# Two-layer graph kernel: transposed exponentials in pairs of groups, a regrouped opening, and other queues and spacing at the start of layer 1

## The chip, the cores and the metric

The kernel runs on one core of one Trainium2 chip. Its engines run side by side and wait for one another by semaphores: TensorE (PE; its weight loads are listed as PEld), VectorE (DVE), ScalarE (ACT), GpSimd (POOL) and SyncE (SP), which here mostly issues DMAs. The metric is the device time of a whole execution in microseconds (us), lower is better.

## What is computed

There are 2708 nodes with 256 features and a dense matrix adj, about as sparse as a random graph. Two layers follow each other, each with a residual and a layernorm. Cut to what matters:

```python
# layer 0, two steps n = 0, 1
A  = softmax(Xa @ W1.T @ W2.T @ (Xa @ W3.T).T)      # N x N
A  = keep the largest entries of each row up to a mass of 0.9, rescale
R  = (adj + I) / row sum
Xf = R @ Xf
Xa = A @ Xa
Z  = Z + Xf @ U1[n].T + Xa @ U2[n].T
h  = layernorm(x + Z) * ln_g + ln_b
x  = layernorm(x + h)
# layer 1, four heads of 64
Wh = x @ W                                          # per head
e  = leaky_relu(s_i[:, None] + s_j[None, :])        # s = Wh @ a, per head
p  = softmax(e where adj or the diagonal is nonzero)
x  = layernorm(x + p @ Wh)
```

All of it is in float32.

## The kernel before

**Tiles.** The 2708 rows are 22 tiles, 16 of 128 rows and 6 of 110. For transposes they are put into six groups: four of four tiles of 128, one of four and one of two tiles of 110 (`groups`, L75).

**The attention of layer 0.** One tile of target rows has its exponentials e in an array of 128 x 2708. To multiply them with the values, each 128 x 128 block has to be turned. `turned` (L235) transposes the blocks of one group on TensorE into a PSUM buffer `tr` (L240) and has ScalarE copy them to `eT` (L245). `weigh` (L248) runs over the six groups of a target tile: it first turns the group after the present one, then issues the present group's matmuls (L258, one for each source tile), then calls `between`, in which all other work is put. After the last group, group 0 of the next target tile is turned. The PSUM pool ps_tr, from which `tr` comes, has two buffers, used in turn, and it is used for other things as well: the turned rows of the next X (L644), the projections to queries and keys (`project`, L631, emptied at L635 and L636), `terms2` (L960, products with U, emptied by ScalarE at L965 and L966), and `sources` (Wh and s for layer 1, L160 to L176). ScalarE thus empties nearly every buffer of ps_tr, in the order of its program.

**What sets the order.** Inside the layers the order is written out by hand: every engine executes its instructions in the order in which the program issues them. `slot` (L999) is called once for each group of each target tile. It advances every running search by one stage (`going`), starts the search of target tile t + 3 at one place of the tile, advances the unfinished follow-up work (`doing`), and then spends some matmuls of the "walks" (R @ Xf, L901). A search computes a tile's scores (L661), its exponentials (L665), tallies over them on ScalarE (L686), and on DVE the threshold of the 0.9 mass, ending with the masked e.

**The stages.**
- Opening: `turn_x` (L1080) turns the groups of x by TensorE into PSUM, in two halves c = 0, 1 of the features (L1086). After each half a copy empties it (L1091), ScalarE for c = 0, DVE for c = 1. `project` (L631) then makes queries and keys of the group. The group after it is turned ahead of each projection. Then come `terms1` for all tiles (L946) and the first searches.
- Step 0: attention of 22 tiles; `spend` is 0, so there are no walks beside it. Follow-up work of a tile is L644, on odd tiles a projection of two tiles, and `terms2`.
- Between: 15 slots (L1117 to L1121) with seven walk matmuls each; the first searches of step 1 are started. The last source of each walk tile sets DVE's sum xf (L915).
- Step 1: attention of 22 tiles with six or seven walk matmuls after each group (SPEND_1, L37). Follow-up work is the layernorms and `sources`, which stores v, the scaled Wh, to memory.
- Layer 1: target tiles in three spans of 8, 8 and 6 tiles, sources j in pairs. `neighbours` (L1214) loads a block of adj and makes a 0/1 mask on ScalarE (Sign L1221, Square L1222). `weights` has DVE make the four heads' products pt (L1302), `values` and `denominators` are the matmuls (L1313, L1323). `mask` (L1286) also loads v of a source tile, in the first span only, through SP's queue (L1290).
- Late tiles: the last four tiles (LATE) are not finished in layer 0. `prepared` (L1330) carries their layernorm and `sources` on beside the first pairs of layer 1. `beside` is called twice for each pair of source tiles; an entry `[k, part]` of `late` lets k calls pass before its first stage, and then does one stage per call. `verdict`, which checks that the threshold search was valid, follows them; a general path behind it is not run.

**Memory.** SBUF tiles come from pools; a pool's place is taken from another's after that is closed. The pools of layer 1 lie where those of layer 0 lay, so their first use waits for the last use of what was there.

Of the kernel before, what the change touches and what calls it, by code (L numbers as in the profile page):

```python
# [8 lines left out]
F32 = mybir.dt.float32  # L9
# [7 lines left out]
P = 128  # L17
# [17 lines left out]


SPEND_BETWEEN, SPEND_1 = 7, (7, 6, 7, 7, 6, 7)  # L37
HELD, WAITING = 6, 4
LN2 = 0.6931471805599453

Z_LOW, Z_HIGH = 1e-25, 1e30
# [3 lines left out]
def kernel(  # L45
# [16 lines left out]
    nc = tc.nc  # L62
    N, D = x.shape
# [4 lines left out]
    NT = (N + P - 1) // P  # L68

    rows = [P] * 16 + [110] * 6  # L70
# [177 lines left out]
    def weigh(acc, ahead, m, value, turn_next, between=None):  # L248

        for n, grp in enumerate(groups):
            eT, ahead = ahead, turn_next(n + 1)
            for q, t in enumerate(grp):
                nc.tensor.matmul(  # L258
                    acc, eT[: rows[t], q, :m], value(t),
                    start=(t == 0), stop=(t == NT - 1),  # L260
                )
            if between:
                between(n)
        return ahead


    def general_layer0():
        with ExitStack() as l0:
# [18 lines left out]
            keep = l0.enter_context(tc.tile_pool(name="keep", bufs=1))  # L287
            ep = l0.enter_context(tc.tile_pool(name="ep", bufs=2))
            wk = l0.enter_context(tc.tile_pool(name="wk", bufs=1))
            tpp = l0.enter_context(tc.tile_pool(name="tpp", bufs=4))  # L290
            adjp = l0.enter_context(tc.tile_pool(name="adjp", bufs=2))
            ps_lg = l0.enter_context(tc.tile_pool(name="ps_lg", bufs=2, space=PSUM))
            ps_tr = l0.enter_context(tc.tile_pool(name="ps_tr", bufs=2, space=PSUM))
# [142 lines left out]
            def attend(t, e, rden, cur, dst):  # L436

                m = rows[t]
                ac = ps_ac.tile([P, CHUNK], F32, name="ac")

                def turn_next(n):
                    return turned(e, m, n, tpp, ps_tr, nc.scalar.copy) if n < len(groups) else None

                weigh(ac[:m, :D], turn_next(0), m, lambda j: cur[: rows[j], j, 0:D], turn_next)
                nc.scalar.activation(dst, ac[:m, :D], AF.Copy, scale=rden[:m])

            def walk(s, t, dst):
# [77 lines left out]
    def fast_layer0(ep, adjp):  # L525

        l0 = ExitStack()

        heldp, finp, rowp, w0, keep, tpp, sortp, keepb, wk = (
            l0.enter_context(tc.tile_pool(name=name, bufs=bufs))  # L530
            for name, bufs in (
                ("heldp", HELD), ("finp", 2), ("rowp", 2), ("w0", 1), ("keep", 1),
                ("tpp", 3), ("sortp", 1), ("keepb", 1), ("wk", 1),
            )
        )
        ps_lg, ps_wk, ps_at, ps_tr = (
# [317 lines left out]
        def walks():  # L854

            queue = [
                (s, t, j0, j1)  # L860
                for s in range(STEPS) for t in range(NT) for j0, j1 in ((0, HT), (HT, NT))
            ]

            def load(s, t, j0, j1):
                m = rows[t]
                blk = adjp.tile([P, NT - HT, P], F32, name="blk")
                if (s, t) < (0, 2):

                    nc.gpsimd.memset(blk[:, :, 0:1], 0.0)
                by_tile(blk[:, :, :m], adjT[:, off[t] : off[t + 1]], j0, j1)  # L870
                return blk

            blocks = [load(*queue[0]), load(*queue[1])]
            yield
            for n, (s, t, j0, j1) in enumerate(queue):
                m = rows[t]
                cur, w = (xe, D + 1) if s == 0 else (xm, D)
                while s and unfinished:
                    yield True
                blk = blocks.pop(0)  # L880
                if n + 2 < len(queue):
                    blocks.append(load(*queue[n + 2]))
                if j0 == 0:
                    ac = ps_wk.tile([P, CHUNK], F32, name="walk")
                    if s and t >= NT - LATE:
                        ca = x_late[:, t - NT + LATE, :]
                        nc.gpsimd.memset(ca[:, 0:1], 0.0)
                    else:
                        ca = finp.tile([P, D], F32, name="ca", bufs=4)
                    if s:  # L890
                        cb = finp.tile([P, D], F32, name="cb")
                        nc.sync.dma_start(ca[:m], x[off[t] : off[t + 1], :])
                        nc.sync.dma_start(cb[:m], c2[t][:m])
                        if t in c3:
                            assert t in stored
                            held[t] = finp.tile([P, D], F32, name="cc")
                            nc.sync.dma_start(held[t][:m], c3[t][:m])
                    else:
                        nc.sync.dma_start(ca[:m], c1[t][:m])
                for j in range(j0, j1):  # L900
                    nc.tensor.matmul(  # L901
                        ac[:m, :w], blk[: rows[j], j - j0, :m], cur[: rows[j], j, 0:w],
                        start=(j == 0), stop=(j == NT - 1),
                    )
                    if j == NT - 1:
                        doing.append(after_walk0(t, ac, ca) if s == 0 else finish(t, ac, ca, cb))
                        next(doing[-1])
                    yield j == NT - 1
# [103 lines left out]
        def step(s, cur, spend):  # L1012
            first = None
            for t in range(NT):
                m = rows[t]
                e, rden = ready[t]
                ac = ps_at.tile([P, CHUNK], F32, name="att")
                if s == 0 and t == NT - 1:
                    next(stream)
                if s and t == NT - 2:  # L1020
                    share(0, ps_tr.tile([P, 4, P], F32, name="tr"))
                if s and t == NT - 1:
                    ahead.extend(room(ep))
                    spread(0, ahead)

                def between(n):
                    last = n == len(groups) - 1
                    if last:
                        xa = heldp.tile([P, D], F32, name="xa1")
                        nc.scalar.activation(xa[:m], ac[:m, :D], AF.Copy, scale=rden)  # L1030
                        if s and t in c3:
                            nc.gpsimd.dma_start(c3[t][:m], xa[:m])
                            stored.add(t)
                        elif s:
                            held[t] = xa
                        else:
                            doing.append(after_attention0(t, xa))
                    slot(spend[n], (s, t + 3) if n == len(groups) - 2 else None)

                def turn_next(n):  # L1040
                    u = t + n // len(groups)
                    if u == NT:
                        return None
                    return turned(ready[u][0], rows[u], n % len(groups), tpp, ps_tr, nc.scalar.copy)

                first = weigh(
                    ac[:m, :D], first or turn_next(0), m,
                    lambda j: cur[: rows[j], j, 0:D], turn_next, between,
                )
                ready.pop(t)  # L1050
# [29 lines left out]
        def turn_x(grp):  # L1080
            k = rows[grp[0]]
            w, c0 = k * len(grp), off[grp[0]]
            tp = ps_lg.tile([P, 2, CHUNK], F32, name="lg")
            for c in range(DC):
                for q, t in enumerate(grp):
                    nc.tensor.transpose(  # L1086
                        tp[:, c, q * k : (q + 1) * k], xm[:k, t, c * P : (c + 1) * P],
                        ident[:k, :k],
                    )
                copy = nc.vector.tensor_copy if c else nc.scalar.copy  # L1090
                copy(x_turned[:, c, c0 : c0 + w], tp[:, c, :w])  # L1091
            return c0, w

        with tc.manual_schedule(engines=engines):
# [22 lines left out]
            for t in range(3):  # L1117
                for n in range(6):
                    slot(SPEND_BETWEEN, None if n else (1, t))
                    if (t, n) == (2, 2):  # L1120
                        break  # L1121
            step(1, ba, SPEND_1)
            owed[0] = 0
# [69 lines left out]
    def layer1(ep, adjp, r=None, verdict=None):  # L1193
        l1 = ExitStack()

        pp, pj, rp, keep = (
            l1.enter_context(tc.tile_pool(name=name, bufs=bufs))
            for name, bufs in (("pp", 2), ("pj", 1), ("rp", 1), ("keep1", 1))
        )
        DEEP = 3  # L1200
        ps_u = l1.enter_context(tc.tile_pool(name="ps_u", bufs=2, space=PSUM))
# [84 lines left out]
        def mask(n):  # L1286
            if n < len(order):
                g, _, j = order[n]
                if g == 0:
                    nc.sync.dma_start(  # L1290
                        v[j][: rows[j]].rearrange("p h o -> p (h o)"), vd[j][: rows[j]]
                    )
                masks[n] = neighbours(g, j)
# [44 lines left out]

        late = []
        if verdict:  # L1340
            late += [[k, prepared(NT - LATE + k)] for k in range(LATE)]
            late.append([LATE, verdict(aux)])
        rest, running = [], []
        def beside(g, i):

# [128 lines left out]
```

## Time and profile before

| | us |
|---|---|
| median of 3 runs | 1595.95 (1595.8 to 1597.88) |
| the profiled execution's own time | 1593.14 |
| its span, first to last instruction | 1591.3 |
| mean granted TensorE clock | 0.990 of full |

Stages of the profiled execution, from the busy time of windows of the trace (us; the limits are read from the timeline):

| stage | window | PE busy | DVE busy | ACT busy |
|---|---|---|---|---|
| opening | 0 to 34 | 20.9 | 8.1 | 6.8 |
| terms1, first searches | 34 to 80 | 46.0 | 30.5 | 22.4 |
| step 0 | 80 to 448 | 366.8 | 248.9 | 157.5 |
| between | 448 to 523 | 69.4 | 40.4 | 36.7 |
| step 1 | 523 to 1229 | 704.4 | 558.7 | 390.6 |
| layer 1, first pairs | 1229 to 1312 | 75.8 | 72.0 | 40.5 |
| layer 1, the rest | 1312 to 1591 | 259.0 | 243.9 | 144.5 |

The waits of TensorE by what ended them, from the view of waits: L1086 for ScalarE's copy L1091 6.4 us in 6 waits; L901 for DVE's L915 5.0 in 3; L166 for ScalarE's L162 3.8 in 2; L1313 for the DMA of v 2.2; L631 for ScalarE's L636 1.6 in 2; L160 for ScalarE's L153 1.1; each of the others is at most 1.0 us, except those for the first weights.

How to read it: a line of the timeline is start, duration, engine, line of the kernel, operation, output<-inputs, shape, count, and in brackets how long the engine had been idle and which instruction released it. Busy times of matmuls overlap (a matmul's record lasts longer than the time to the next one's start), so times per matmul are taken from start to start. Two records stand for each float32 matmul.

### The profile page before, as it was taken

The numbers are of one execution on the slowest core, as the hardware profiler recorded it, in microseconds if no ns is written. First come the engines' busy times: TensorE is split into PE (matmuls) and PEld (weight loads), VectorE is DVE, ScalarE is ACT, GpSimd is POOL, SyncE is SP. The second block draws the span as 40 slices with busy tenths as digits, with TensorE's granted clock in tenths as the row PEclk, the third lists the DMA queues.
The fourth block names the chain that finished last, engine by engine and source line by source line (L and its number), as shares of the span: only waits on it lengthen the run. The fifth ranks groups of instructions, "written<-read, shape, count | busy, mean of one in ns | idle before, by whom it ended". The sixth has DMA issues, their size and how long they took to land. (4 is left out here: it accounts for less than half of the span.)

```text
span 1591.3 us, 23822 instructions
## 1 busy us (share of the span) xinstructions
PE 1542.3 (97%) x8029; PEld 1037.7 (65%) x8029; DVE 1202.5 (76%) x3651; ACT 798.9 (50%) x1462; POOL 429.1 (27%) x884
## 2 busy tenths in 40 slices
PE   6999999999998999999999999999999999999994
PEld 3477777777776888787787788887787333333342
DVE  2777677767408876878779888888884978999995
ACT  2444444444335455555555556556643454456473
POOL 1311000000022222232224454534441720033133
PEclk9999999999999999999999999999999999999997
DMA  5200000000134333333333334433344434334331
GB/s 139 78 13 14 12 9 12 10 9 10 42 94 124 86 100 82 98 76 78 80 102 94 100 107 107 111 104 93 78 101 130 130 102 139 93 105 133 85 100 43
DMA packets 172494, 128.27 MB, mean 81 GB/s; under 512 B 44342, under 2 KB 161804, under 8 KB 172362
## 3 DMA queue, kind: packets, MB, share of 16 engines
q1 hardware_dynamic: 165030, 114.63, 26.9%
q0 software_dynamic: 3648, 9.26, 1.8%
q10 hardware_dynamic: 3684, 2.76, 0.5%
q8 instruction: 65, 1.06, 0.3%
q14 instruction: 67, 0.55, 0.1%
HBM read 111.78 MB, written 13.46 MB: 79 GB/s over the span
## 5 line engine op out<-in xcount | busy, mean ns | idle before, releaser
L245 ACT COPY eT<-tr 128x512 f32<-128x512 f32 (+5 forms) x264 | 141.2, 535 | 275.8 <-PE tr L240 273.1
L686 ACT ACTIVATE junk<-e,minus,rth 128x2708 bf16<-128x2708 f32 (+1 forms) x88 | 232.8, 2646 | 36.1 <-POOL rth L718 35.2
L258 PE MATMUL att<-xm,eT 128*128 128x256 f32 (+3 forms) x968 | 230.9, 380 | 0.4 <-ACT xa L1030 0.4
L258 PE MATMUL att<-ba,eT 128*128 128x256 f32 (+3 forms) x968 | 230.8, 379 | 0.3 <-ACT eT L245 0.2
L901 PE MATMUL walk<-xe,blk 128*128 128x257 f32 (+3 forms) x968 | 225.3, 384 | 5.0 <-DVE xf L915 5.0
L901 PE MATMUL walk<-xm,blk 128*128 128x256 f32 (+3 forms) x968 | 222.0, 380 | 1.0 <-DVE xw L974 1.0
L1313 PE MATMUL acc<-pt,v 128*64 128x512 f32 (+3 forms) x1056 | 216.3, 555 | 2.4 <-DMA v<-v 2.2
L901 PEld LDWEIGHTS walk<-xe,blk 128*128 128x128 f32 (+3 forms) x968 | 178.5, 187 | 50.3 <-issue 12.6
L1302 DVE SCALAR_TENSOR_TENSOR pt<-e,tj,blk 128x1024 f32<-128x1024 f32 (+3 forms) x176 | 187.1, 1128 | 20.3 <-PE att L258 8.7
L901 PEld LDWEIGHTS walk<-xm,blk 128*128 128x128 f32 (+3 forms) x968 | 177.7, 186 | 34.5 <-issue 4.9
L258 PEld LDWEIGHTS att<-xm,eT 128*128 128x128 f32 (+3 forms) x968 | 169.6, 186 | 22.1 <-ACT xa L1030 0.8
L258 PEld LDWEIGHTS att<-ba,eT 128*128 128x128 f32 (+3 forms) x968 | 169.5, 186 | 22.0 <-ACT eT L245 0.8
L665 ACT ACTIVATE e<-lg 128x1024 f32<-128x1024 f32 (+1 forms) x132 | 121.0, 921 | 110.6 <-PE lg L661 107.0
L1313 PEld LDWEIGHTS acc<-pt,v 128*64 128x64 f32 (+1 forms) x1056 | 75.6, 139 | 133.2 <-issue 107.5
L766 DVE MAX8 cand<-e 128x8 f32<-128x170 f32 (+1 forms) x352 | 89.6, 323 | 90.5 <-ACT e L665 90.4
L240 PEld LDWEIGHTS tr<-ident,e 128*128 128x128 f32 (+3 forms) x968 | 115.1, 138 | 56.3 <-issue 21.0
L240 PE MATMUL tr<-ident,e 128*128 128x128 f32 (+3 forms) x968 | 147.1, 271 | 0.7 <-ACT xe L952 0.3
L1302 DVE SCALAR_TENSOR_TENSOR pt<-r,tj,blk 128x1024 f32<-128x1024 f32 (+1 forms) x88 | 110.0, 1313 | 5.8 <-PE acc L1323 3.0
L1323 PE MATMUL acc<-pt,sb 128*32 128x512 f32 (+3 forms) x1056 | 106.8, 545 | 0.0
L766 DVE MAX8 cand<-scr 128x8 f32<-128x97 f32 (+1 forms) x616 | 102.3, 245 | 0.0
L1221 ACT ACTIVATE blk<-blk 128x1024 f32<-128x1024 f32 (+3 forms) x66 | 63.1, 956 | 70.2 <-DMA blk<-in_adjT_dram 57.1
L915 DVE TENSOR_TENSOR xf<-walk,xe 128x257 f32<-128x257 f32 (+1 forms) x22 | 9.4, 426 | 110.8 <-PE walk L901 110.8
(237 smaller groups left out, 1976.2 us busy)
## 6 DMA issues: line engine op xcount, KB each, us to landing
blk<-in_adjT_dram SPq DMA_DIRECT2D x32, 704.0 KB
blk<-in_adjT_dram SPq DMA_DIRECT2D x32, 512.0 KB
blk<-in_adjT_dram SPq DMA_DIRECT2D x48, 330.0 KB
blk<-in_adjT_dram SPq DMA_DIRECT2D x32, 320.0 KB
blk<-in_adjT_dram SPq DMA_DIRECT2D x12, 605.0 KB
blk<-in_adjT_dram SPq DMA_DIRECT2D x12, 440.0 KB
blk<-in_adjT_dram SPq DMA_DIRECT2D x18, 283.6 KB
c<-cs POOLq DMA_DIRECT2D x32, 128.0 KB, 2.0
```

The lines of the kernel that those rows point to most:

```text
L240: nc.tensor.transpose(tr[: rows[t], q, :m], e[:m, off[t] : off[t + 1]], ident[:m, :m])
L245: copy(eT[:k, : len(grp), :m], tr[:k, : len(grp), :m])
L258: nc.tensor.matmul(acc, eT[: rows[t], q, :m], value(t), start=(t == 0), stop=(t == NT - 1),)
L665: nc.scalar.activation(halves[:m, :, c0 : c0 + w], lg[:m, :, :w], AF.Exp, accum_out=zp[:m, n : n + 1],)
L686: nc.scalar.activation(junk[:m], e[:m], func, scale=rth, bias=minus1[:m], accum_out=acc)
L766: nc.vector.max(cand[:, n, :], src[:m, n * size : min(N, (n + 1) * size)])
L901: nc.tensor.matmul(ac[:m, :w], blk[: rows[j], j - j0, :m], cur[: rows[j], j, 0:w], start=(j == 0), stop=(j == NT - 1),)
L915: nc.vector.tensor_add(xf[:m], ac[:m, : D + 1], xe[:m, t, :])
L1221: nc.scalar.activation(bar, bar, AF.Sign)
L1302: nc.vector.scalar_tensor_tensor(pt[:k, :gw], targets[g][h // 2][:k, h % 2, :gw], tj[:k, j, h : h + 1], bar, op0=ALU.max, op1=ALU.mult,)
L1313: nc.tensor.matmul(acc[h // 2][c][q * FO : (q + 1) * FO, :w], v[j][:k, h, :], probs[n][h][:k, c0 : c0 + w], **at,)
L1323: nc.tensor.matmul(acc[2][c][h * 32 : (h + 1) * 32, :w], sb[:k, j, h : h + 1].to_broadcast([k, 32]), probs[n][h][:k, c0 : c0 + w], **at,)
```

## The change

It does six things.

1. `weigh` turns two groups at once: at every even n the groups n + 2 and n + 3, while the matmuls use the two that were turned before. The order on TensorE is thus eight transposes, a group's matmuls and its `between`, the next group's matmuls and its `between`. Both callers pass a list of two. The pool tpp (eT) has four buffers instead of three; ps_tr keeps two. HELD is 5 instead of 6, and `ca` has three buffers instead of four.
2. Searches of t + 3 begin at group len(groups) − 3 instead of len(groups) − 2, and the between phase has 16 slots instead of 15.
3. `turn_x` issues the transposes of both halves before both copies.
4. Layer 1 loads v through ScalarE's queue instead of SP's.
5. The late tiles start 2k calls of `beside` late instead of k, and the verdict 2 * LATE instead of LATE.
6. The order of pools in memory changes: tpp stands after rowp in layer 0, and rp before pj in layer 1.

```diff
-HELD, WAITING = 6, 4
+HELD, WAITING = 5, 4
...
         for n, grp in enumerate(groups):
-            eT, ahead = ahead, turn_next(n + 1)
+            if n % 2 == 0:
+                now, ahead = ahead, [turn_next(n + 2), turn_next(n + 3)]
+            eT = now[n % 2]
             for q, t in enumerate(grp):
                 nc.tensor.matmul(
...
-        heldp, finp, rowp, w0, keep, tpp, sortp, keepb, wk = (
+        heldp, finp, rowp, tpp, w0, keep, sortp, keepb, wk = (
             l0.enter_context(tc.tile_pool(name=name, bufs=bufs))
             for name, bufs in (
-                ("heldp", HELD), ("finp", 2), ("rowp", 2), ("w0", 1), ("keep", 1),
-                ("tpp", 3), ("sortp", 1), ("keepb", 1), ("wk", 1),
+                ("heldp", HELD), ("finp", 2), ("rowp", 2), ("tpp", 4), ("w0", 1),
+                ("keep", 1), ("sortp", 1), ("keepb", 1), ("wk", 1),
             )
         )
...
-                        ca = finp.tile([P, D], F32, name="ca", bufs=4)
+                        ca = finp.tile([P, D], F32, name="ca", bufs=3)
...
-                    slot(spend[n], (s, t + 3) if n == len(groups) - 2 else None)
+                    slot(spend[n], (s, t + 3) if n == len(groups) - 3 else None)
...
-                    ac[:m, :D], first or turn_next(0), m,
+                    ac[:m, :D], first or [turn_next(0), turn_next(1)], m,
                     lambda j: cur[: rows[j], j, 0:D], turn_next, between,
...
-                copy = nc.vector.tensor_copy if c else nc.scalar.copy
+            for c, copy in enumerate((nc.scalar.copy, nc.vector.tensor_copy)):
                 copy(x_turned[:, c, c0 : c0 + w], tp[:, c, :w])
...
-                    if (t, n) == (2, 2):
+                    if (t, n) == (2, 3):
                         break
...
-        pp, pj, rp, keep = (
+        pp, rp, pj, keep = (
             l1.enter_context(tc.tile_pool(name=name, bufs=bufs))
-            for name, bufs in (("pp", 2), ("pj", 1), ("rp", 1), ("keep1", 1))
+            for name, bufs in (("pp", 2), ("rp", 1), ("pj", 1), ("keep1", 1))
         )
...
-                    nc.sync.dma_start(
+                    nc.scalar.dma_start(
                         v[j][: rows[j]].rearrange("p h o -> p (h o)"), vd[j][: rows[j]]
                     )
...
-            late += [[k, prepared(NT - LATE + k)] for k in range(LATE)]
-            late.append([LATE, verdict(aux)])
+            late += [[2 * k, prepared(NT - LATE + k)] for k in range(LATE)]
+            late.append([2 * LATE, verdict(aux)])
```

The general path, which is not run, gets the same form of `weigh` (tpp there with five buffers).

More of the change, by code (lines that the diff above doesn't have):

```diff
@@ L289, in general_layer0 @@
             wk = l0.enter_context(tc.tile_pool(name="wk", bufs=1))
-            tpp = l0.enter_context(tc.tile_pool(name="tpp", bufs=4))
+            tpp = l0.enter_context(tc.tile_pool(name="tpp", bufs=5))
             adjp = l0.enter_context(tc.tile_pool(name="adjp", bufs=2))
@@ L442, in turn_next @@
                     return turned(e, m, n, tpp, ps_tr, nc.scalar.copy) if n < len(groups) else None
-                weigh(ac[:m, :D], turn_next(0), m, lambda j: cur[: rows[j], j, 0:D], turn_next)
+                weigh(ac[:m, :D], [turn_next(0), turn_next(1)], m, lambda j: cur[: rows[j], j, 0:D], turn_next)
                 nc.scalar.activation(dst, ac[:m, :D], AF.Copy, scale=rden[:m])
```

## The prediction

> **What bounds the kernel now.** I read the page's first part, then its groups with the idle time before them, then the timeline stage by stage. The page (columns of the groups: busy us, mean ns | idle before, releaser):
>
> ```profile
> span 1591.3 us, 23822 instructions
> PE 1542.3 (97%) x8029; PEld 1037.7 (65%) x8029; DVE 1202.5 (76%) x3651; ACT 798.9 (50%) x1462; POOL 429.1 (27%) x884
> ...
> L258 PE MATMUL att<-ba,eT 128*128 128x256 f32 (+3 forms) x968 | 230.8, 379 | 0.3 <-ACT eT L245 0.2
> ...
> L240 PE MATMUL tr<-ident,e 128*128 128x128 f32 (+3 forms) x968 | 147.1, 271 | 0.7 <-ACT xe L952 0.3
> ```
>
> TensorE is the bound nearly everywhere. The attention matmuls (L258) wait 0.3 us in all for the transposed exponentials eT: one group ahead already covers that copy. The means of 271 and 379 ns are latencies of overlapped records; from start to start a transpose takes 0.109 us and an L258 or L901 matmul 0.43 (two records), and the step from L240 to L258 and back costs no more. So pairing two groups of transposes cannot save TensorE work. What can change is the waits. Those before are in three places. The opening (timeline: start, duration, engine, line [idle before]):
>
> ```profile
> 16.97 0.58 ACT L636 COPY qT<-tr 64x512 f32<-64x512 f32 x1 [5.34 <-DVE junk L635]
> 17.57 0.58 ACT L1091 COPY ba<-lg 128x512 f32<-128x512 f32 x1
> ...
> 18.21 0.66 PE L1086 MATMUL lg<-ident,xm 128*128 128x128 f32 x4 [1.18 <-ACT ba L1091]
> ...
> 22.58 0.66 PE L1086 MATMUL lg<-ident,xm 128*128 128x128 f32 x4 [1.56 <-ACT ba L1091]
> ...
> 34.10 1.99 PE L661 MATMUL lg<-junk,qT 64*128 64x512 f32 x8
> ```
>
> The second half of a group's transposes waits for ScalarE's copy of the first half. The period is 22.58 − 18.21 = 4.37 us, of which TensorE works 2.60.
>
> Layer 1's first pairs of source tiles (TensorE, then ScalarE, then SP):
>
> ```profile
> 1231.49 10.48 PE L1313 MATMUL acc<-pt,v 128*64 128x512 f32 x32 [2.19 <-DMA v<-v]
> ...
> 1256.06 7.09 PE L1313 MATMUL acc<-pt,v 128*64 128x512 f32 x32
> ...
> 1267.86 0.41 PE L160 MATMUL aux<-ident,xe 110*128 110x110 f32 x2 [1.15 <-ACT xe L153]
> ...
> 1282.18 1.14 PE L166 MATMUL aux<-wx,xT 128*110 128x264 f32 x4 [2.05 <-ACT xT L162]
> ...
> 1298.74 1.14 PE L166 MATMUL aux<-wx,xT 128*110 128x264 f32 x4 [1.74 <-ACT xT L162]
> ```
> ```profile
> 1224.78 1.06 ACT L1222 ACTIVATE blk<-blk 128x1024 f32<-128x1024 f32 x1
> ...
> 1229.34 0.47 ACT L1030 ACTIVATE xa<-att,rden 110x256 f32<-110x256 f32 x1 [2.25 <-PE att L258]
> ```
> ```profile
> 1229.33 4.67 SPq L1290 DMA_DIRECT2D v<-v  x10
> ```
>
> The third place is the between phase: 0.52, 1.32 and 3.18 us of waits for DVE's xf (L915).
>
> In step 0 there is nearly no wait. How tight it is shows here (TensorE, then ScalarE):
>
> ```profile
> 309.45 1.88 PE L960 MATMUL tr<-u_sb,xT 128*128 128x512 f32 x4
> 311.17 0.60 PE L240 MATMUL tr<-ident,e 128*128 128x128 f32 x4
> ```
> ```profile
> 311.37 0.37 ACT L965 COPY cs<-tr 128x256 f32<-128x256 f32 x1 [2.81 <-PE tr L960]
> 311.64 0.38 ACT L966 COPY ba<-tr 128x256 f32<-128x256 f32 x1
> ```
>
> ScalarE has emptied the PSUM buffer of terms2 (L960) only at 312.02, 0.85 us after the next transposes began.
>
> **The skill.** "TensorE: Matmul & The Clock Gate", Part 1, says that an idle window of about 3.4 us leaves the array at half rate until a busy one has passed. The trace agrees: half-clock stretches of 3.413 us at 1232.0, 1283.2 and 1300.3 follow waits. Part 4 there says a transpose goes to PSUM and needs a copy; here L245, 535 ns. "PSUM — Partial Sum Buffer", Engine vs sequencer instructions, says ScalarE is strict FIFO and matmuls start in program order, so a waiting transpose holds every matmul behind it, and a copy waits behind whatever ScalarE has queued; the 1.18 us above are of this kind. "DMA: Bandwidth & Descriptors", Issuing engines are not separate DMA queues, says another issuer saves only issue time; that loads go faster from ScalarE is thus not expected, and no trace of before shows these loads there.
>
> **The change part by part** (sum against the profiled execution's 1593.14 us, span 1591.3; the median 1595.95 is 2.81 above, and I carry the difference over).
>
> *Opening, −8.2 (−7 to −8.8).* Without the wait a period is 8 × 0.109 + 4 × 0.43 = 2.60 us. From the first transpose at 7.25, with the clock at half as before: T0 1.74, T1 1.74, P0 3.46, to 14.2; then at full rate T2 0.87, P1 1.73, T3 0.87, P2 2.17 (two pieces), T4 0.87, P3 1.73, T5 0.22 to 0.44, P4 and P5 2.40: the scores (L661) start at about 25.3 instead of 34.10; if the half rate lasts until 16.86 as it did, at about 27. DVE's copies now follow ScalarE's: 0.68 + 0.58 + 0.58 + 0.69 = 2.53 us from the end of one projection to the input of the next but one, which has 3.47. x's transfers end near 11 us. Nothing later eats this: the first tile's search ends at 52.85 and is used at 80.01.
>
> *Step 0, +10.6 (+7 to +13).* ps_tr keeps two buffers. At n = 2 the two transposed groups T4 and T5 now follow directly on terms2 (even tiles) or project (odd tiles) in the order of the built program: T4 takes the free buffer, T5 the one that terms2 or project filled, with only T4's four transposes (0.44) between. There are 11 places of the one kind and 10 of the other. Terms2: from the start of its last matmul the copies end after 1.28 us in every tile; T5 could start after 0.43 + 0.44 = 0.87; 0.41 plus about 0.11 for the semaphore and the exposed weight load is 0.53. Project: q's copy (L636) ends 1.16 after, T5 could start 0.65 after: 0.51 + 0.1 = 0.6. So 11 × 0.53 + 10 × 0.6 = 11.8. Before, a group's four attention matmuls, 1.73 us, were additional cover for the same wait. Gone are the three waits of a short last group's copy, 0.35 + 0.35 + 0.41 = 1.1, which two groups now cover. Bounds: all places at 0.35, and all at 0.65.
>
> *Between phase, −0.4 (−1.9 to +1.1).* The break one slot later starts seven walk matmuls (3 us) earlier, and they are missing at step 1's end; their number is the same, 968 per kind. Only which matmul meets DVE's xf can move: half a wait either way.
>
> *Step 1, +1.5 (−1 to +6).* Searches begin one group earlier; the list DVE must finish before the pair is turned is shifted alike (slack before 2 to 10 us). The second group of a pair waits for the evacuations L176 and L162, which on ScalarE may stand behind a tally (L686, 2.65 us each). I find five places in the built order with seven walks or fewer as cover; 0.3 on average is 1.5. No row of before shows such a pair; below nothing it cannot go by more than the step's own 0.49 + 0.21 + 0.96 + 0.34 of waits. ca with 3 buffers and held with 5 still load more than a walk ahead: nothing. The pools' new order moves memory only: nothing by itself.
>
> *Layer 1's start, +2.1 (+1.5 to +3.5).* The v loads go to ScalarE's queue. Before, the masks (L1221, L1222) of the first three tiles ran at 1206.9 to 1225.8, under the attention. Now, in the built order, the first v load stands behind the last xa (L1030) and the masks behind it. So the first pt starts at E + 0.5 (xa) + 0.3 to 0.57 (issue, as L179 measured) + 2.12 (mask) = E + 3.1 with E = 1229.30, and not at E + 0.10. TensorE waited until E + 2.19 for v anyway and then ran beside DVE's products; the first pair ends at about E + 14.7 where it ended at E + 12.6. The later masks have cover: 10.6 us of TensorE per pair.
>
> *Late tiles at every second pair, −6.9 (−3 to −8.4).* From 1245.47 to 1312.43 five pairs took 66.96 us. Undisturbed they take 5 × 10.59 = 52.95, the prepared tiles' own matmuls (4 L160 pairs, 4 L166 at 0.98) some 5.3. The rest, 8.7, is the waits 1.15 + 2.05 + 1.74 and two half-clock stretches at 1.7 each. With 2k no two L166 of neighbouring tiles stand back to back, and xT's copy has a pair's matmuls to hide in. I leave 1.5 for a remaining wait of the L153 kind.
>
> Sum: −8.2 + 10.6 − 0.4 + 1.5 + 2.1 − 6.9 = −1.3: 1591.8 on the profiled execution's scale, 1594.6 on the median's.
>
> **Rivals.** *Faster:* the outer gains come in full and step 1 gives nothing back: −8.5 + 10.6 − 1.9 + 0 + 1.5 − 8.4 = −6.7, or 1589. For it: both gains rest on waits that are printed in the trace. Against: the edges of every bound at once. *Slower, the two PSUM buffers in step 1:* besides the five places, the other 17 tiles lose half a microsecond as in step 0, because ScalarE has a 2.65 us tally ahead of L176 or L162: 17 × 0.5 = +8.5, to 1603. It decides from 4.5 us on (0.2 per tile). For it: ScalarE once holds a copy for 9.5 us at 893.7 (a tally waiting for POOL), and now two groups and not one wait for it. Against: walks of seven matmuls, 3 us, mostly stand between. *Slower, layer 1:* the later masks on ScalarE make DVE late for several pairs, and the late tiles, spread over nine pairs, give waits again: late −1, start +5, hence +7.5, or 1603.5. For it: mask, layernorm and v issue share a FIFO. Against: ScalarE works 40.5 of 83 us there. *The pairing doesn't do what it says:* there is no switching cost to save, as shown; that is inside the forecast.
>
> **How the numbers follow.** About 0.2% (3.2 us) is what a measurement can tell from no change. Forecast, within 0.2%: 0.37. Faster: 0.33, since the forecast lies on that side and the two gains are the best measured. Slower: 0.20 by PSUM in step 1, 0.10 by layer 1. The forecast alone reaches from 1592.8 to 1599; the range to both sides of the cases is 1587.5 to 1603.
>
> **What would show it.** The first L661 at 25 to 27; 21 waits of L240 on ScalarE's copies in step 0, some 0.5 each; eT waits still nil; the first L1313 later relative to the last L258; no half clock between layer 1's second and sixth pair. It is wrong if L240 waits little in step 0, or over 5 us in step 1, or if pairs of layer 1 lengthen beyond 10.6 us.

## The result, and the profile after

The changed kernel takes 1613.52 us (median of 4 runs, 1613.3 to 1615.7); the kernel before 1595.88 (4 runs). The ratio is 1.0112, with a 95% interval of 1.0094 to 1.0129: slower by 1.1%. Between the two profiled executions the difference is 20.4 us (own times 1613.56 and 1593.14). The first lines of the page of the changed kernel, and the group that has changed most (columns as before):

```profile
span 1611.7 us, 23813 instructions
## 1 busy us (share of the span) xinstructions
PE 1547.8 (96%) x8029; PEld 1044.3 (65%) x8029; DVE 1202.6 (75%) x3651; ACT 793.3 (49%) x1462; POOL 444.9 (28%) x884
...
L240 PE MATMUL tr<-ident,e 128*128 128x128 f32 (+3 forms) x968 | 131.7, 272 | 19.1 <-ACT cs L176 6.1
```

TensorE does the same 8029 matmuls. The transposes, which waited 0.7 us in all, now wait 19.1. What they wait for is in the view of waits (us in total, times, longest):

```profile
PE aux L160 <- ACT xe L153: 6.5, 3, 2.2
PE tr L240 <- ACT cs L176: 6.1, 4, 5.1
...
PE tr L240 <- ACT xT L162: 4.7, 4, 2.5
PE acc L1315 <- DVE pt L1304: 4.1, 1, 4.1
PE tr L240 <- ACT qT L638: 3.9, 10, 0.5
PE tr L240 <- ACT ba L968: 3.5, 11, 0.4
```

All of these L240 lines are waits for ScalarE to empty a PSUM buffer. To see where the 20.4 us lie, I take the start times of the same matmuls in both traces:

| stage, by start of its first and last matmul | before | after | difference | forecast |
|---|---|---|---|---|
| opening, to the first score (L661, after L663) | 34.10 | 25.10 | −9.0 | −8.2 |
| from there to the first attention matmul | 47.35 | 48.68 | +1.3 | |
| step 0, first to last attention matmul | 367.13 | 378.27 | +11.1 | +10.6 |
| from there to step 1's first (between) | 76.22 | 79.82 | +3.6 | −0.4 with step 1's +1.5 |
| step 1, first to last attention matmul | 704.13 | 714.63 | +10.5 | |
| layer 1's first matmul | 2.57 | 4.49 | +1.9 | +2.1 |
| first pair of sources | 13.98 | 14.05 | +0.1 | |
| next nine pairs (late tiles) | 110.47 | 111.45 | +1.0 | −6.9 |
| the rest | 235.40 | 235.21 | −0.2 | 0 |

The +1.3 ahead of step 0 comes with the pairing: this stage takes 47.35 us in a1 and b1 below and 48.68 in d2. The slot added to the between phase holds seven walk matmuls, 3.0 us, which are then missing in step 1; between and step 1 together lose 14.1. Two steps are far off: these, and the late tiles.

**Step 0** looks as drawn beforehand. TensorE, then ScalarE:

```profile
308.48 1.88 PE L962 MATMUL tr<-u_sb,xT 128*128 128x512 f32 x4
310.19 0.60 PE L240 MATMUL tr<-ident,e 128*110 128x128 f32 x4
311.09 0.43 PE L240 MATMUL tr<-ident,e 128*110 128x128 f32 x2 [0.30 <-ACT ba L968]
```
```profile
310.66 0.38 ACT L968 COPY ba<-tr 128x256 f32<-128x256 f32 x1
```

The first group's four transposes go at 310.19 into the free buffer. The second group needs the buffer of L962, which ScalarE leaves at 311.04; it starts at 311.09, where 310.63 would have been its place. The printed wait (0.30) counts from the modelled end of the transpose before; from start to start 0.46 is lost.

**Step 1**, the longest wait (timeline, TensorE and ScalarE with one GpSimd line):

```profile
896.24 1.05 PE L166 MATMUL tr<-wx,xT 128*128 128x264 f32 x4
...
899.72 0.60 PE L240 MATMUL tr<-ident,e 128*110 128x128 f32 x4
...
901.36 0.19 POOL L720 TENSOR_TENSOR rth<-rth,g 128x1 f32<-128x1 f32 x1
...
901.59 2.64 ACT L688 ACTIVATE junk<-e,minus,rth 128x2708 bf16<-128x2708 f32 x1 [7.97 <-POOL rth L720]
...
904.41 0.93 ACT L176 ACTIVATE cs<-tr,sb 128x64 f32<-128x64 f32 x4
...
905.39 0.67 PE L240 MATMUL tr<-ident,e 128*110 128x128 f32 x2 [5.08 <-ACT cs L176]
```

L166's result lies in PSUM from 897.3 on. ScalarE would copy it (L176), but a tally (L688) stands before that in its order, and this waits for GpSimd's rth until 901.55. The copy ends at 905.3. In the kernel before the same delay was there (its tally began at 899.49), but a group of attention matmuls and two sets of walks stood between L166 and the transposes that needed its buffer, which waited 0.32 us:

```profile
903.29 0.43 PE L240 MATMUL tr<-ident,e 128*110 128x128 f32 x2 [0.32 <-ACT cs L176]
```

Now the second group of the pair stands at the head of TensorE, and attention and walks behind it. The second longest wait of L240 is of the same kind, a copy (L162) behind a tally that waits 4.25 us for GpSimd:

```profile
1184.82 0.40 PE L240 MATMUL tr<-ident,e 110*110 110x110 f32 x2 [2.54 <-ACT xT L162]
```

The windows of the trace show what comes after (columns: us, busy time and count of PE, PEld, DVE, ACT, POOL, then PEclk, DMA share, GB/s):

```profile
896.20:905.20 9.00, 4.12 (x21) 3.35 (x20) 8.69 (x28) 3.61 (x9) 5.86 (x14) 1.00 0.41 104
905.20:908.60 3.40, 3.21 (x9) 2.67 (x10) 2.59 (x5) 3.11 (x4) 3.32 (x2) 0.50 0.11 39
1185.10:1188.50 3.40, 3.40 (x11) 2.46 (x10) 3.40 (x5) 3.07 (x4) 0.00 (x0) 0.50 0.65 164
```

For 3.4 us TensorE has half its clock, here and after the wait of 2.5 us. Records of L260 then start every 0.43 us and not every 0.22, so each stretch costs about 1.7 us more (an estimate, half its length).

**The late tiles** (TensorE, then ScalarE):

```profile
1299.02 1.14 PE L166 MATMUL aux<-wx,xT 128*110 128x264 f32 x4
1302.36 0.41 PE L160 MATMUL aux<-ident,xe 110*128 110x110 f32 x2 [2.19 <-ACT xe L153]
```
```profile
1300.41 0.93 ACT L176 ACTIVATE cs<-aux,sb 110x64 f32<-110x64 f32 x4
1301.36 0.29 ACTq L179 DMA_DIRECT2D v<-cs  x1
1301.70 0.60 ACT L153 ACTIVATE xe<-h,lb_nb,lb_rs 110x256 f32<-110x256 f32 x1 [0.37 <-ACT cs L176]
```

L166 of one tile is directly followed by L160 of the next. L160 waits for L153, and this stands on ScalarE behind the copies of the L166 that has just run. It happens three times.

### The profile page after: what moved, and what is told of

Read it like the earlier page. It is cut to its first block, busy times and chain, and to the rows that moved or that the text cites. A ratio compares the mean times of both kernels' runs of the same rounds, so it can differ in the third digit from the quotient of the medians.

```text
span 1611.7 us, 23813 instructions
## 1 busy us (share of the span) xinstructions
PE 1547.8 (96%) x8029; PEld 1044.3 (65%) x8029; DVE 1202.6 (75%) x3651; ACT 793.3 (49%) x1462; POOL 444.9 (28%) x884
## 5 line engine op out<-in xcount | busy, mean ns | idle before, releaser
L688 ACT ACTIVATE junk<-e,minus,rth 128x2708 bf16<-128x2708 f32 (+1 forms) x88 | 233.1, 2648 | 70.3 <-POOL rth L720 69.4
L260 PE MATMUL att<-ba,eT 128*128 128x256 f32 (+3 forms) x968 | 233.1, 383 | 0.0
L260 PE MATMUL att<-xm,eT 128*128 128x256 f32 (+3 forms) x968 | 230.5, 382 | 0.0
L1315 PE MATMUL acc<-pt,v 128*64 128x512 f32 (+3 forms) x1056 | 215.6, 554 | 4.4 <-DVE pt L1304 4.1
L1304 DVE SCALAR_TENSOR_TENSOR pt<-e,tj,blk 128x1024 f32<-128x1024 f32 (+3 forms) x176 | 185.5, 1121 | 24.1 <-ACT blk L1224 18.6
L260 PEld LDWEIGHTS att<-xm,eT 128*128 128x128 f32 (+3 forms) x968 | 171.5, 186 | 36.3 <-issue 14.0
L260 PEld LDWEIGHTS att<-ba,eT 128*128 128x128 f32 (+3 forms) x968 | 176.6, 188 | 26.4
L245 ACT COPY eT<-tr 128x512 f32<-128x512 f32 (+5 forms) x264 | 130.9, 539 | 102.7 <-PE tr L240 100.5
L1315 PEld LDWEIGHTS acc<-pt,v 128*64 128x64 f32 (+1 forms) x1056 | 76.5, 138 | 132.7 <-issue 111.5
L240 PE MATMUL tr<-ident,e 128*128 128x128 f32 (+3 forms) x968 | 131.7, 272 | 19.1 <-ACT cs L176 6.1
L240 PEld LDWEIGHTS tr<-ident,e 128*128 128x128 f32 (+3 forms) x968 | 108.2, 139 | 58.7 <-issue 21.0
L786 DVE MAX8 top<-work 128x8 f32<-128x128 f32 (+3 forms) x242 | 82.4, 341 | 8.3
```

The lines of the kernel that those rows point to most:

```text
L240: nc.tensor.transpose(tr[: rows[t], q, :m], e[:m, off[t] : off[t + 1]], ident[:m, :m])
L245: copy(eT[:k, : len(grp), :m], tr[:k, : len(grp), :m])
L260: nc.tensor.matmul(acc, eT[: rows[t], q, :m], value(t), start=(t == 0), stop=(t == NT - 1),)
L688: nc.scalar.activation(junk[:m], e[:m], func, scale=rth, bias=minus1[:m], accum_out=acc)
L786: nc.vector.max(top[:, k : k + 8], work if k else flat)
L1304: nc.vector.scalar_tensor_tensor(pt[:k, :gw], targets[g][h // 2][:k, h % 2, :gw], tj[:k, j, h : h + 1], bar, op0=ALU.max, op1=ALU.mult,)
```

## The experiments

Single totals of the kernel before went from 1590.4 to 1599.7 us over the experiments' runs, so the stages of the profiled executions carry the arguments, and medians with intervals the totals. Totals without a ratio are of one execution. Steps 0 and 1 repeat well: in the five kernels that leave them alone (before, b1, b4, c1, d1) step 0 takes 367.13 to 367.14 us and step 1 704.12 to 704.47. The nine pairs of layer 1 (the expectations call them ten pairs) do not: with the late tiles as before they take 110.47 us (before), 108.81 (d2) and 114.15 (b1).

**The pairing alone undone (a1_unpaired).**

```diff
-            if n % 2 == 0:
-                now, ahead = ahead, [turn_next(n + 2), turn_next(n + 3)]
-            eT = now[n % 2]
+            eT, ahead = ahead, turn_next(n + 1)
```

> The changed kernel with the pairing alone undone (one group turned ahead; searches still begin at group len - 3, 16 slots between, the opening, the v queue and the late spacing as changed). Theory P, two PSUM buffers: the 11 us that step 0 lost and some 12 of the 14 us that step 1 lost go, so about 1590 us, and L240's waits for L638, L968, L176 and L162 fall from 18 us in all to under 2. Rival S, the earlier start of the searches, which puts tallies ahead of ScalarE's copies: step 1 keeps its loss, about 1602.

Measured: 1595.93 us, ratio to before 1.0008 (1.0000 to 1.0016). L240 waits 0.3 us in all for L176 and not at all for L162, L638 and L968, and step 1 takes 701.84 us, 12.8 less than with the pairing: rival S is out. The total is 6 us over the expectation because step 0 keeps 7.5 us of its loss (374.63 against 367.13). Its cause is another one. With the searches one group earlier, no scores stand between the last attention matmul of one tile and the first transposes of the next, and the next tile's first attention matmul has to wait until L1030 has emptied the one accumulator (TensorE, then ScalarE):

```profile
264.01 0.60 PE L240 MATMUL tr<-ident,e 128*128 128x128 f32 x4
264.74 2.00 PE L258 MATMUL att<-xm,eT 128*128 128x256 f32 x8
```
```profile
264.22 0.47 ACT L1030 ACTIVATE xa<-att,rden 128x256 f32<-128x256 f32 x1 [0.16 <-PE att L258]
```

From the one start to the other it is 0.73 us in 21 tiles, where before it is 0.73 in two tiles and at most 0.49 in the others. All steps from transposes to attention together are 5.6 us longer than before; another 1.9 lie in the first group of attention matmuls of each tile (1.82 us and not 1.73), whose cause stays open. With the pairing eight transposes stand in this place, 0.75 to 0.88 us, which covers the accumulator. So the earlier search and the pairing belong together in step 0.

**A third buffer in step 0 (a2_third_buffer).** The second group of a pair goes to the bank of the walks, which step 0 does not use:

```diff
-        tr = ps.tile([P, 4, P], F32, name="tr")
+        if spare is None:
+            tr = ps.tile([P, 4, P], F32, name="tr")
+        else:
+            tr = spare.tile([P, CHUNK], F32, name="walk").rearrange("p (a b) -> p a b", b=P)
...
+                        ps_wk if s == 0 and n % 2 else None,
```

> The changed kernel, but in step 0 the second group of each pair is transposed into the PSUM bank of the walks, which is idle there: a third buffer, no other order. Theory P: step 0 from the first to the last attention matmul returns to the kernel before or up to 1 us less (11.2 us less than with the change), about 1602 us. Rival, that the eight transposes in a row themselves cost (weight loads, the switch): step 0 stays at 11 us over before, about 1613.

Measured: step 0 takes 366.46 us, the whole 1601.18. The same place as above, TensorE of this kernel:

```profile
301.70 1.88 PE L965 MATMUL tr<-u_sb,xT 128*128 128x512 f32 x4
303.42 0.60 PE L243 MATMUL tr<-ident,e 128*110 128x128 f32 x4
303.85 0.38 PE L243 MATMUL walk<-ident,e 128*110 128x128 f32 x2
```

The second group follows after 0.43 us, the four transposes' own time. Eight in a row cost nothing; step 0's 11.8 us are the two buffers.

**The second group turned after the first group's matmuls (a3_split).**

```diff
-                now, ahead = ahead, [turn_next(n + 2), turn_next(n + 3)]
+                now, ahead = ahead, [turn_next(n + 2)]
...
+            if n % 2 == 0:
+                ahead.append(turn_next(n + 3))
             if between:
                 between(n)
```

> The changed kernel, but the second group of a pair is turned after the first group's matmuls and not before them; still two groups ahead, two buffers. Theory P: each wait for a buffer gets 1.7 us more cover, so step 0's waits (0.3 to 0.5 each) all go, 11 us, and of step 1's long waits (5.1, 2.5, 1.5) some 1.7 each go with the small ones, 7 to 9 us: about 1593 to 1596. Rival S: step 0 as in P, but step 1 keeps 12 to 14 us, about 1602.

Measured: 1602.48 us; step 0 375.13, step 1 707.00. Of the buffer waits of step 0 none is left, but as in a1 the accumulator's wait takes their place (the same step takes 0.73 us in 21 tiles, in all 6.4 us over the 0.44 or 0.38 that four transposes take). The waits of 5.1 and 2.5 us in step 1 fall to 3.4 and 1.4, by 1.7 and 1.1 us. The expectation for the total missed the accumulator; that for step 1 held.

**Late tiles in reversed order (a4_late_reversed).**

```diff
-            for part in list(late):
+            for part in reversed(list(late)):
```

> The changed kernel, but the parts of the late tiles are advanced from the last to the first, so that the next tile's normalisation L153 stands on ScalarE ahead of the copies L170 to L176 that wait for this tile's L166. Theory F, ScalarE's order: the three waits of L160 for L153 (2.2, 2.2, 2.1) go, about 1607 us. Rival, that the work at the seam of two pairs of source tiles is too close together whatever the order: a wait of about 2 us reappears at L166 or L160, 1612 to 1614.

Measured: 1611.66 us; the nine pairs 110.28 instead of 111.45. The three waits at this seam go, as Theory F has it, but L160 of the first late tile now waits 3.3 us for L153, which a GpSimd step had held up (below), and another 1.1 for a buffer. A gain of 1.2, not 6.5: both sides of the expectation hold a part.

**The opening alone (b1_opening_only)**: the kernel before with part 3 of the change.

> The kernel before with the opening alone changed (the transposes of both halves ahead of both copies). If the step was priced rightly and nothing later eats it: the first scores at 25 us instead of 34.1, the first attention matmul 7.7 us earlier, and all of that at the end: 1595.0 - 7.7 = about 1587 us, faster. Rival, that a later wait takes it back: 1593 to 1596.

Measured: 1584.01 us, ratio 0.9930 (0.9906 to 0.9953): faster. The first score is at 25.61, the first attention matmul 8.5 us earlier than before, and step 0 (367.14) and step 1 (704.28) are as they were. The step was priced rightly, and steps 0 and 1 take none of it back. In the profiled execution layer 1 takes back 3.7 us: the nine pairs last 114.15 us instead of 110.47, with the long GpSimd step described at the end. That execution, 1588.46, is the slowest of the four; the other three took 1581.2 to 1585.5.

**v on SP's queue (b2_v_on_sp)**: the changed kernel with `nc.sync.dma_start` for v.

> The changed kernel with the v loads back on SP's queue, all else as changed. Theory Q, the queue: the first masks run under the last attention again, TensorE waits about 2.2 us at the start of layer 1 and not 4.1, and the GpSimd step of 13 us (L149 at 1260.7, which holds ScalarE's normalisation and the masks behind it until 1274.7) is back at about 1 us, so that layer 1's third pair loses its 1.9: about 4 us less, 1609 to 1610. Rival M, the order of the pools in memory: the 13 us step stays, only the start gains: 1611 to 1612.

Measured: 1613.47 us. Layer 1's first matmul comes after 2.60 us and not 4.49, as both theories have it, but the nine pairs take 113.60 instead of 111.45, and the total is the same. The GpSimd step is still there, with 11.9 us. Theory Q is out, and so is M: in b1 the same step takes 12.1 us with the old order of pools.

**The late spacing alone (b4_late_only)**: the kernel before with part 5.

> The kernel before with the late tiles' spacing alone changed (2k and 2 * LATE). As predicted: layer 1 from its second to its eleventh pair takes 104 us instead of 110.5 and the whole is about 1588. Theory F, the seam: `beside` at the end of one pair and at the start of the next have no matmul between them, so L166 of one tile and L160 of the next stand side by side; three waits of about 2 us for L153 take the place of the two of L166 and the one of L160: the stage takes 109 to 111 us, 1593 to 1596.

Measured: 1596.9 us; the nine pairs 111.22, where 110.47 was before. Theory F holds in its mechanism (stage and total lie 0.2 and 0.9 us above its ranges). From the view of waits:

```profile
PE aux L160 <- ACT xe L153: 6.8, 3, 2.5
```

The waits of L166 (3.8 us in two) are gone, and this is in their place. The difference of 0.75 us is smaller than that between two traces with the old spacing (110.47 and 108.81), so it is no loss that is shown; what is shown is that the gain is missing.

**Opening, 2k and reversed (c1_open_late_rev)**: the kernel before with these three edits.

> The kernel before with the opening changed, the late tiles at 2k, and their parts advanced from the last to the first; v on SP, no pairing, searches and slots as before. Theory F: L160's waits for L153 go as well, the stage of ten pairs takes 103 to 106 us, and with the opening's 7.7 the whole is 1580 to 1583. Rival, that waits reappear at the same seam: 1586 to 1588, no better than the opening alone.

Measured: 1581.01 us, ratio 0.9906 (0.9880 to 0.9932); the nine pairs 108.27. The total is as Theory F had it, the stage 2.3 us over its range. As in a4 one long wait for L153 stays (3.6 us).

**Opening, 2k and two calls of slack (d1_open_late_slack).**

```diff
             yield from norms(
                 t, x_late[:, t - NT + LATE, :], layernorm_beside,
                 lambda: pp.tile([P, D], F32, name="h2", bufs=4),
             )
+            yield
+            yield
             yield from sources(t, pp, aux, nc.scalar)
```

> The kernel before with the opening changed, the late tiles at 2k, and two more calls of `beside` between a late tile's second normalisation and its transposes, so that L153 of a tile stands on ScalarE ahead of the copies that wait for the tile before, and has a pair of source tiles to hide in. Theory F: no wait of L160 for L153 is left, ten pairs of layer 1 take 103 to 105 us (108.3 with the parts reversed, 111.2 with 2k alone, 110.5 before), and the whole is 1575 to 1580. Rival, that GpSimd's long step decides: the stage stays at 107 to 109, 1580 to 1583.

Measured: 1577.36 us, ratio 0.9906 (0.9889 to 0.9922), the lowest median of all versions; the ratio is the same as c1's. The nine pairs take 103.15. TensorE at the seam:

```profile
1279.67 1.14 PE L166 MATMUL aux<-wx,xT 128*110 128x264 f32 x4
1280.65 0.35 PE L160 MATMUL aux<-ident,xe 110*128 110x110 f32 x2
1280.93 7.09 PE L1313 MATMUL acc<-pt,v 128*64 128x512 f32 x32
```

L166 and L160 stand side by side as before, and neither waits, since L153 now is on ScalarE ahead of L166's copies. At the next two seams 1.1 and 1.0 us of waits for L176 remain, which empties a buffer of the PSUM pool aux.

**The pairing alone (d2_pairing_only)**: the kernel before with parts 1 and 2.

> The kernel before with the pairing alone and what belongs to it (tpp 4, HELD 5, ca 3, searches from group len - 3, 16 slots). Theory P: what the paired kernel loses against the unpaired one is the pairing's own, so step 0 takes 378 us (367 before), step 1 714 to 716 (704 before) with L240 waiting 18 us in all, and the whole is 1616 to 1621. Rival, that opening and layer 1 had a part in it: step 1 under 710, the whole under 1612.

Measured: 1617.06 us; step 0 378.31, step 1 714.07, L240's waits 18.6 us in five rows. The loss is the pairing's own.

**The second group in a buffer of the scores' pool (d3_pairs_own_bank)**: the changed kernel, with a2's edit but `spare.tile([P, 2, CHUNK], F32, name="lg")[:, 0]` and

```diff
+                        ps_lg if n % 2 else None,
```

> The changed kernel, but the second group of each pair is transposed into a buffer of the scores' PSUM pool, in both steps: more buffers, the same order of instructions on every engine. Theory P: step 0 falls from 378 to 366 to 368 us as with the walks' bank, step 1 from 714.6 to 701 to 706, L240's waits from 18 us to under 3, and the whole is 1589 to 1593. Rival, that in step 1 ScalarE's late copies hold the matmuls whatever the buffer (eT itself comes late): step 1 stays over 711, the whole about 1601.

Measured: 1587.58 us; step 0 367.49, step 1 700.23. In this trace the transposes into the two pools stand in two groups:

```profile
L245 PE MATMUL tr<-ident,e 128*128 128x128 f32 (+3 forms) x528 | 78.3, 270 | 0.0
L245 PE MATMUL lg<-ident,e 128*128 128x128 f32 (+3 forms) x440 | 68.6, 270 | 0.0
```

No transpose waits any more, with ScalarE, GpSimd and the order of instructions as in the changed kernel. HELD, `ca`, tpp, the searches and the slots are those of the changed kernel too, so none of these has a part in it. The price of two buffers in step 1 is 714.63 − 700.23 = 14.4 us: the 10.8 us of waits and about 3.4 from two stretches at half clock.

**The best version with the pairing (e1_best_with_pairs)**: d1 with parts 1 and 2 and d3's buffer.

> The kernel with the changed opening, 2k and two more calls before the transposes of a late tile, to which the pairing is added with the scores' PSUM pool for the second group of each pair. It tells whether turning two groups at once is worth anything once it has its buffers. Theory P: the copies were covered before, so nothing is gained: step 0, between and step 1 together 1145 to 1147 us (1146.3 without the pairing), the whole 1576 to 1579. Rival, that the pairing brings a gain which the buffer wait only hid: 1570 to 1574.

Measured: 1581.55 us, ratio 0.9918 (0.9899 to 0.9938). Step 0, between and step 1 together, measured as in the table above, take 1146.8 us, 1147.5 without the pairing (d1): theory P. The total is 4 us over d1's and above the expected 1576 to 1579, all of it in layer 1's first pairs (107.33 against 103.15), where the long GpSimd step came again.

## Why the prediction was wrong, point by point

The forecast was 1594.6 with a range to 1603; 1613.5 is outside. Of its steps four were right in mechanism and size: the opening (−9.0, 0.2 beyond its range; b1 alone shows 8.5), step 0 (+11.1), the start of layer 1 (+1.9), and that pairing has no work of TensorE to save (e1).

**The step that failed first is step 1, "+1.5 (−1 to +6)".** The mechanism was named, the size was not: "five places in the built order with seven walks or fewer as cover; 0.3 on average". The trace has eight waits, four for L176 and four for L162, with 10.8 us, of which three (5.1, 2.5, 1.5) make 9.1; over 5 was the prediction's own sign of being wrong. I had counted how many places had short cover and gave each a small mean, where most of the sum comes from two places at which a tally waiting for GpSimd stands ahead of the copy (5.1 and 2.5; at the third the tally runs without such a wait). Such a delay was in the profile of before and in my text (ScalarE holds a copy for 9.5 us at 893.7); I put it into a rival, and that rival's price, 17 × 0.5, was again a mean of small waits. The place of 893.7 is the 5.1 us wait. The half clock after it, 3.4 us in the two places, was in no bound. d3 shows that it is all the buffers' doing, and d2 that it is all the pairing's.

**The second is the late tiles, "−6.9 (−3 to −8.4)".** The failing sentence is that with 2k xT's copy "has a pair's matmuls to hide in" and that 1.5 us remain. The first half came true: L166 waits no more. But I treated the calls of `beside` as evenly spaced. Matmuls lie between the call at a pair's start and the call at its end; between that and the next pair's start there are none. With 2k, every L166 falls on the end of a pair and the next tile's L160 on the start of the following one, and L153 stands behind L166's copies on ScalarE. I had looked at what TensorE has between the two and not at what ScalarE has. b4 has the step alone at +0.75, no change within what this stage varies. In the changed kernel the third pair loses 1.9 us to the GpSimd step below (12.80 us, 10.93 in b4), while b4 has 6.8 us at half clock at 1283.8, where the changed kernel has 3.4 at 1331.9.

**The v loads** were priced rightly at their place, but undoing them gains nothing in the sum: b2 gives the 1.9 us back at the start and loses 2.1 in the pairs after. Whether the queue or this stage's own variation costs the 2.1 is not shown. That a gain at the entrance of a stage is not carried through it, I had checked for the opening and not here.

Of the rivals, the PSUM one was the right story, at a chance of 0.20 and too cheap: with it, between and step 1 would have cost −0.4 + 1.5 + 8.5 = 9.6 us, and they cost 14.1. The late tiles' 7.9 us come on top. The other one, of layer 1, happened in half of its form: the start was not late by 5 us, but the late tiles gave waits again.

The Trainium skill's page "TensorE: Matmul & The Clock Gate", Part 1, says that an idle window of about 3.4 us leaves the array at half rate, and the prediction found the trace in agreement. The traces agree on how long the half rate lasts, 3.4 us or twice that, and not on the idle time ahead of it: in the changed kernel the wait of 2.5 us was followed by it, and so were, in the kernel before, the waits of 2.19, 2.05 and 1.74 us. It does not follow each such wait, either. The waits of 2.2 us at 1302 and 1316 and those of 1.5 us and less in step 1 were not followed by it, and d2, with the same waits of 5.1 and 2.5 us in step 1, has 6.8 us of half clock after the first and none after the second. I had used the page to price a gain (late tiles) and not to price a loss.

## What to carry to other kernels

Before work is issued further ahead, count the buffers it passes through: moving a second group up to the first takes away the work that covered its PSUM buffer, and it then waits for whatever the emptying engine has in its order, at worst for a chain over three engines. Price such a wait by the longest delays that the emptying engine shows in the trace, with a stretch of half clock that may follow, and not by a mean over places. Where work is spread by calls of a helper, write down what each engine has between two calls; here two calls with nothing between them put a copy ahead of the instruction that the next call needed.

## What was not expected of the hardware

In nine of the fourteen traces (the changed kernel, a1 to a4, b1, b2, d3, e1) one GpSimd instruction on 110 x 1 elements, L149, takes 11.9 to 13.0 us, and in c1 another (L146) 7.3; in the others (before, b4, d1, d2) L149 takes 0.7 to 0.9 us at that place. GpSimd, VectorE and ScalarE of the changed kernel:

```profile
1260.74 12.97 POOL L149 TENSOR_SCALAR lb_sq<-lb_sq 110x1 f32<-110x1 f32 x1 [6.11 <-ACT h L148]
```
```profile
1249.66 24.01 DVE L1304 SCALAR_TENSOR_TENSOR pt<-e,tj,blk 128x1024 f32<-128x1024 f32 x20 [13.06 <-ACT blk L1224]
```
```profile
1274.67 0.60 ACT L153 ACTIVATE h<-xe,lb_nb,lb_rs 110x256 f32<-110x256 f32 x1 [9.34 <-POOL lb_nb L151]
```

VectorE's twenty products stand back to back and end at 1273.66; the GpSimd step ends at 1273.71. In all nine traces it ends 0.05 us after the last product of such a series (0.09 in c1). It looks like a circle: ScalarE's L153 waits for GpSimd, the next masks stand behind L153, and VectorE pauses because the masks are missing; only with that pause does the GpSimd step end. "SBUF — State Buffer", SBUF: two separate sides, describes the pair of ports that VectorE and GpSimd share as an exclusive lock for one whole instruction. A hold over ten VectorE instructions is more than that sentence says, and that the ports are the cause here is not shown. In d1 VectorE runs forty products without a pause, and the same GpSimd instruction takes 0.67 us among them (GpSimd, then VectorE):

```profile
1233.26 0.67 POOL L149 TENSOR_SCALAR lb_sq<-lb_sq 110x1 f32<-110x1 f32 x1 [7.65 <-ACT h L148]
```
```profile
1220.90 51.72 DVE L1302 SCALAR_TENSOR_TENSOR pt<-e,tj,blk 128x1024 f32<-128x1024 f32 x40 [8.67 <-PE att L258]
```

What decides which of the two happens is open, and was not tried. The long step costs the third pair 1.9 us in the changed kernel (its 32 records of L1315 take 8.96 us and not 7.09) and 3.7 in b1 (the pair takes 15.82 us, 12.14 before), and it is a part of the few microseconds by which totals of layer 1 differ between kernels with the same instructions there.
